# A graph attention kernel: two picked tiles in every batch from three bfloat16 parts, in place of one and two in turns from float32

## The chip, the core and the metric

The kernel runs on one core of a Trainium2 chip. The metric is the device time of one execution in microseconds (us), as the median of several runs; less is better. The profile is of one execution. The engines are named as the profile names them: PE is TensorE's matmuls and PEld its weight loads, DVE is VectorE, ACT is ScalarE, POOL is GpSimd, and SP is SyncE, which only issues DMAs.

## The reference

Three layers of a graph transformer on 6250 nodes of 64 numbers and 206250 directed edges (each edge in both directions and a loop at every node), sorted by their destination. Every edge has 64 numbers of its own. One layer is

```
def _transformer_conv(x, src, dst, edge_attr, Wq, bq, Wk, bk, Wv, bv, We, Ws, bs):
    q = x @ Wq + bq
    k = x @ Wk + bk
    v = x @ Wv + bv
    e = edge_attr @ We
    kj = k[src] + e
    alpha = jnp.sum(q[dst] * kj, axis=-1) / jnp.sqrt(jnp.float32(D))
    amax = jax.ops.segment_max(alpha, dst, num_segments=N)
    p = jnp.exp(alpha - amax[dst])
    denom = jax.ops.segment_sum(p, dst, num_segments=N)
    w = p / denom[dst]
    msg = (v[src] + e) * w[:, None]
    agg = jax.ops.segment_sum(msg, dst, num_segments=N)
    return agg + x @ Ws + bs

for i in range(L):                       # L = 3
    x = _transformer_conv(x, src, dst, edge_attr, Wq[i], bq[i], ...)
    x = jax.nn.relu(x)
    if i < L - 1:
        x = _layer_norm(x, ln_gamma[i], ln_beta[i])
return jax.nn.log_softmax(x, axis=1)
```

and the output is the layer norm of the input plus this. Everything is float32.

## The kernel before

**Tiles.** The edges are padded to 403 chunks of 512 (`CH`), each of four tiles of 128 edges (`T`). Four chunks are a batch (`LB`), so a batch has sixteen tiles and there are 101 batches, the last with three chunks. The nodes are 49 blocks (`NB`) of 128 rows. A batch lives in one buffer `feat` of six (`FB`): per edge the 64 numbers of the source node and the 64 of the edge. The edge half comes by one DMA on SP's queue (`fetch`). The node half is gathered: for each tile POOL issues one indirect DMA (`gather`, L542) that reads 128 rows of the layer's input from DRAM by the edges' sources.

**Picked tiles.** Some tiles at the end of a batch are not gathered but picked out of a copy of all node rows in SBUF (`xins`, 49 blocks of 128 rows in float32) by products with zeros and ones. `PICKS = (1, 2)`: batches pick one tile and two tiles in turns, beginning with batch 4 in the first layer. `keys` splits each source number into a key, which tells the bank of eight blocks and the row in a block, and the block within the bank. `aim` (L740) spreads one or two tiles' keys over all partitions by a product into the PSUM buffer `ps_p` (L746), and DVE compares them with the seven banks' row numbers (L751, seven operations) into the 0/1 matrices `hot`. `pick` (L754) then makes seven products a tile, one a bank, of 128 by 128 by 512 (the last one 64 wide), which add up in a PSUM buffer `ps_x` of two (L764); DVE keeps the right block of eight by a mask (L774) and a sum (L777), which writes the tile into `feat`. A float32 product shows in the profile as two matmuls, each with its own weight load.

**A round.** The main loop (L1127) is written out by hand and does one batch a round; each engine runs its instructions in the order in which they are issued there. In round u PE does: the sums of batch u-2 (`sums`, L1026, 32 matmuls of 32 columns), after which the buffer is free and POOL gathers batch u+4 into it (`room`); the transposed weights of batch u-1 (`weights`, L1018); the scores of batch u (`scores`, L999 and L1001), whose maximum DVE takes (L1006) and whose exponentials ACT makes (L1010); then the transposes of batch u+1's chunks in four turns (`turn`, L993 on PE, L994 on ACT into `featT`, six buffers). Between the turns stand the parts of `pick` for batch u+1, up to the fourth of the seven products after the first turn and the rest after the second, the same for a second tile around the third turn, and the `aim` for batch u+2 between the first two parts.

**Node work.** A generator is advanced by one step after every turn (`step`). `finish` (L855) closes a group of four blocks when all its edges are done: it merges two partial tables, multiplies by the value weights, normalises, stores the rows for the next layer's gathers and ends with `project` (L803) for the next layer, which makes the scaled queries (L812, L819), the skip part (L817) and a bias column (L824). In the first layer `begin` (L832) runs `project` on the input rows, which three DMAs (`enter`) load into `xins[0]` at the start. There are 13 groups in each layer. At a layer's end the node work is run out and POOL gathers the next layer's first six batches in a row.

Of the kernel before, what the change touches and what calls it, by code (L numbers as in the profile page):

```python
# [9 lines left out]
F32 = mybir.dt.float32  # L10
# [7 lines left out]
P = 128  # L18
D = 64
# [14 lines left out]
PICKS = (1, 2)  # L34
# [379 lines left out]
def main_path(  # L414
# [51 lines left out]

    nc = tc.nc
# [38 lines left out]
    xins = [inputs.tile([P, NB, D], F32, name="xin")]  # L506
    start = inputs.tile([P, NB, D], F32, name="xin").rearrange("p b d -> p (b d)")
    MOST = max(PICKS)

    def picked(layer, k):  # L510

        return PICKS[k % len(PICKS)] if batches[k][1] == LB and (layer or k >= LEAD) else 0

# [19 lines left out]
    def gather(layer, k):  # L533
# [3 lines left out]
        for c in range(m):  # L537
            for t in range(T):
                if m == LB and c * T + t >= LB * T - picked(layer, k):
                    continue  # L540
# [13 lines left out]
    assert NK * CH + 2 * NC <= NB * D  # L554
# [24 lines left out]
    def enter(b0, b1):  # L579
        nc.sync.dma_start(xins[0][:, b0:b1], x[b0 * P : b1 * P, :].rearrange("(j p) d -> p j d", p=P))  # L580

    enter(0, GS)
    enter(GS, 2 * GS)
    for k in range(FB):
        fetch(0, k)
        gather(0, k)
        if k == 1:
            enter(2 * GS, NB)
# [114 lines left out]
    keyT = const.tile([NT, MOST * P], F32, name="keyT")  # L703
    which = const.tile([P, MOST, NT, KB], BF16, name="which")
# [3 lines left out]
    def keys():  # L708
# [3 lines left out]
        key = turns.tile([P, MOST, NT], F32, name="key")  # L712
        low = turns.tile([P, MOST, NT], F32, name="low")
        h = turns.tile([P, 2, MOST, NT], F32, name="bits_of")
        tiles = src_b[:, : NT * LB * T].rearrange("p (k t) -> p t k", t=LB * T)
        nc.vector.tensor_copy(key, tiles[:, LB * T - MOST :, :])
# [17 lines left out]
        for s in range(MOST):  # L734
            nc.tensor.transpose(pt[:NT, s * P : (s + 1) * P], key[:, s, :], ident)
        nc.vector.tensor_copy(keyT, pt[:NT, : MOST * P])
# [3 lines left out]
    def aim(layer, k):  # L740

        if k >= len(batches) or not picked(layer, k):
            return
        n = picked(layer, k) * P
        pk = ps("p")[:, :n]
        nc.tensor.matmul(  # L746
            pk, ident[:NT, k : k + 1].to_broadcast([NT, P]), keyT[:, MOST * P - n :], start=True, stop=True
        )
        hot = picks.tile([P, NH, MOST * P], F32, name="hot")
        for h in reversed(range(NH)):  # L750
            nc.vector.tensor_scalar(hot[:, h, :n], pk, rank[:, h : h + 1], None, ALU.is_equal)  # L751
        hots[layer, k] = hot

    def pick(layer, k):  # L754

        if k >= len(batches) or not picked(layer, k):
            return
        hot = hots.pop((layer, k))
        n = picked(layer, k)
        for s in range(n):  # L760
            px = ps("x").rearrange("p (b d) -> p b d", b=KB)
            for h in range(NH):
                b0, b1 = h * KB, min((h + 1) * KB, NB)
                nc.tensor.matmul(  # L764
                    px[:, : b1 - b0, :].rearrange("p b d -> p (b d)"),
                    hot[:, h, s * P : (s + 1) * P],
                    xins[layer][:, b0:b1, :].rearrange("p b d -> p (b d)"),
                    start=(h == 0),
                    stop=(h == NH - 1),
                )  # L770
# [4 lines left out]
                rows, px, which[:, MOST - n + s, k, :].unsqueeze(2).to_broadcast([P, KB, D]), ALU.mult  # L775
            )
            nc.vector.tensor_reduce(  # L777
                loaded[layer, k][:, LB - 1, T - n + s, :D], rows.rearrange("p b d -> p d b"), AX.X, ALU.add
# [24 lines left out]
    def project(layer, g, n, y):  # L803

        pt = ps("a")
# [3 lines left out]
        nc.vector.tensor_copy(xT[:, : n * P], pt[:D, : n * P])  # L809
        yield  # L810
# [3 lines left out]
        nc.scalar.activation(qT[:, : n * P], pq[:D, : n * P], AF.Identity, bias=bqT[:, layer : layer + 1])  # L814
        pk = ps("g")[:, : n * (D + 1)].rearrange("p (j c) -> p j c", j=n)
# [7 lines left out]
        for j in range(n):  # L823
            nc.tensor.matmul(  # L824
                pk[:, j, D:], qT[:, j * P : (j + 1) * P], bkT[:, layer : layer + 1], start=True, stop=True
            )
        nc.vector.tensor_tensor(
# [4 lines left out]
    def begin(g, n):  # L832
        yield from project(0, g, n, xins[0][:, g : g + n])
# [21 lines left out]
    def finish(layer, g, n):  # L855
# [50 lines left out]
        if layer < L - 1:  # L906
            if g == 0:
# [326 lines left out]
```

## Time and profile before

| | |
|---|---|
| median of 3 runs | 7203.82 us (7203.37 to 7209.48) |
| the profiled execution's own time | 7203.82 us |
| its span, first to last instruction | 7202.1 us |
| mean granted TensorE clock | 0.831 |
| gathers by POOL, L542 | 4392 of 0.95 us each, one every 1.25 us |
| picked tiles, L774 | 444, with 6216 matmuls L764 |
| HBM read and written | 354.73 MB and 43.76 MB, 55 GB/s |

The profile gives for each engine the time in which it was busy. For a group of instructions it gives the line, engine, operation, what it writes and reads, the shapes, how many, the busy time in us, the mean of one in ns, and behind the bar the time for which the engine sat idle just before them and what ended most of that. "issue" means that nothing in the profile explains the wait, "remote" that its cause isn't in it. A timeline lists instructions in order of time (start, duration, engine, line), neighbours of one kind merged with their number (x8), and in brackets the idle time before them. A table of windows gives for each stretch its length, then for PE, PEld, DVE, ACT and POOL the busy time and the number of instructions, then the granted TensorE clock, the DMA engines' busy share and GB/s.

### The profile page before, as it was taken

Reading aid. Unit: us, or ns where it says so; the run is one execution under the profiler, and the core shown is the slowest. Engines: PE = TensorE matmul, PEld = TensorE weight load, DVE = VectorE, ACT = ScalarE, POOL = GpSimd, SP = SyncE. Lnnn points to the kernel's source line nnn. Section 1 sums busy time; section 2 is a strip of 40 time slices with the busy share of each in tenths; the row PEclk is TensorE's granted clock in tenths of the full one; section 3 lists DMA queues with packets and bytes.
Section 4 is the critical chain, followed back from the end, with each engine's and each line's share of the span. In section 5 each row is a group of like instructions: output and inputs, shape, how many; then the busy total and the mean of one; then the engine's idle time right before and its main releaser. Section 6 shows DMA issues by size and latency. Waiting matters only on the chain.

```text
span 7202.1 us, 83902 instructions
## 1 busy us (share of the span) xinstructions
PE 5175.8 (72%) x26605; PEld 2701.0 (38%) x26605; DVE 2315.1 (32%) x5431; ACT 1149.7 (16%) x2439; POOL 4165.8 (58%) x4400
## 2 busy tenths in 40 slices
PE   3877777777777657677777777774777777777776
PEld 2433333343333323333333343342333333333333
DVE  1433333333333223333333333331333333333333
ACT  0111111111111111111111111110111111111112
POOL 4455556566656355556656565535666666666663
PEclk9788888888888778888888888876888888888888
DMA  4322222222222212222222222221222222222222
GB/s 97 74 57 54 56 56 58 54 58 59 58 55 54 50 35 57 55 54 58 59 54 57 54 58 56 56 58 26 57 56 57 59 56 56 57 57 56 57 60 42
DMA packets 1098276, 404.43 MB, mean 56 GB/s; under 512 B 923557, under 2 KB 1022395, under 8 KB 1097826
## 3 DMA queue, kind: packets, MB, share of 16 engines
q1 hardware_dynamic: 941250, 246.60, 16.1%
q0 software_dynamic: 140544, 144.20, 10.5%
q10 hardware_dynamic: 16032, 8.17, 0.4%
q8 instruction: 216, 3.54, 0.2%
q14 instruction: 234, 1.92, 0.1%
HBM read 354.73 MB, written 43.76 MB: 55 GB/s over the span
## 4 chain that ended last, share of the span: by engine, by line


## 5 line engine op out<-in xcount | busy, mean ns | idle before, releaser
L542 POOL DMA_INDIRECT feat<-x,src_b x2750 | 2606.7, 948 | 1733.1 <-PE ps_g L1026 941.2
L764 PE MATMUL ps_x<-xin,hot 128*128 128x512 f32 x6216 | 2588.5, 560 | 49.3 <-issue 41.0
L542 POOL DMA_INDIRECT feat<-in_x,src_b x1375 | 1305.9, 950 | 957.6 <-PE ps_g L1026 560.9
L1026 PE MATMUL ps_g<-feat,probT 128*32 128x128 f32 x9672 | 814.9, 333 | 1362.5 <-issue 1335.3
L764 PEld LDWEIGHTS ps_x<-xin,hot 128*128 128x128 f32 x6216 | 1164.7, 197 | 1246.9 <-issue 1238.8
L994 ACT COPY featT<-ps_a 128x512 f32<-128x512 f32 x1209 | 677.4, 584 | 4378.8 <-remote 3335.0
L751 DVE TENSOR_SCALAR hot<-ps_p,rank 128x128 f32<-128x128 f32 (+1 forms) x2072 | 700.6, 409 | 1752.2 <-PE ps_a L993 709.6
L1026 PEld LDWEIGHTS ps_g<-feat,probT 128*32 128x32 f32 x9672 | 439.0, 127 | 1676.0 <-issue 1643.2
L774 DVE TENSOR_TENSOR rows_of_b<-ps_x,which 128x512 f32<-128x512 f32 x444 | 305.9, 689 | 2045.8 <-remote 1899.7
L993 PE MATMUL ps_a<-ident,feat 128*128 128x128 f32 x4836 | 767.0, 288 | 25.8 <-issue 25.8
L993 PEld LDWEIGHTS ps_a<-ident,feat 128*128 128x128 f32 x4836 | 587.4, 152 | 418.1 <-issue 365.3
L1001 PE MATMUL ps_s<-featT,q 128*32 128x512 f32 x2418 | 496.2, 840 | 126.7 <-ACT featT L994 65.0
L777 DVE TENSOR_REDUCE feat<-rows_of_b 128x64 f32<-128x512 f32 x444 | 460.2, 1037 | 15.3
L1010 ACT ACTIVATE prob<-ps_s,part 128x512 f32<-128x512 f32 (+2 forms) x306 | 210.2, 687 | 993.1 <-PE ps_a L993 359.7
L1018 PE MATMUL ps_p<-ident,prob 128*128 128x128 f32 (+2 forms) x1224 | 302.0, 394 | 23.0 <-ACT prob L1010 13.5
L1006 DVE TENSOR_REDUCE most<-ps_s 128x1 f32<-128x512 f32 (+2 forms) x306 | 210.4, 688 | 290.5 <-PE ps_s L1001 288.3
L542 POOL DMA_INDIRECT feat<-x,src_a x174 | 164.2, 943 | 232.6 <-PE ps_a L812 180.1
L1020 DVE COPY probT<-ps_p 128x512 f32<-128x512 f32 (+2 forms) x306 | 207.0, 676 | 190.8 <-PE ps_p L1018 189.6
L1018 PEld LDWEIGHTS ps_p<-ident,prob 128*128 128x128 f32 (+2 forms) x1224 | 195.2, 197 | 124.6 <-issue 48.4
L807 PE MATMUL ps_a<-ident,xin 128*64 128x128 f32 x147 | 38.1, 410 | 205.1 <-DVE xin L853 196.2
L999 PE MATMUL ps_s<-to,codeT 24*128 24x512 bf16 (+2 forms) x306 | 164.5, 537 | 4.2 <-issue 4.2
L1001 PEld LDWEIGHTS ps_s<-featT,q 128*32 128x32 f32 x2418 | 64.7, 128 | 271.9 <-issue 182.8
(123 smaller groups left out, 1706.3 us busy)
## 6 DMA issues: line engine op xcount, KB each, us to landing
feat<-in_ea SPq DMA_DIRECT2D x300, 512.0 KB
feat<-x,src_b POOLq DMA_INDIRECT x2750
feat<-in_x,src_b POOLq DMA_INDIRECT x1375
part<-part SPq DMA_DIRECT2D x1209, 16.2 KB
q<-qq SPq DMA_DIRECT2D x1209, 16.0 KB
both<-part SPq DMA_DIRECT2D x66, 260.0 KB
qq<-qs SPq DMA_DIRECT2D x33, 256.0 KB
to<-places SPq DMA_DIRECT2D x300, 24.0 KB
```

What stands on the lines that cost most here:

```text
L542: nc.gpsimd.indirect_dma_start(out=feat[:, c, t, :D], out_offset=None, in_=xts[layer][:, :], in_offset=bass.IndirectOffsetOnAxis(ap=index[ ...
L751: nc.vector.tensor_scalar(hot[:, h, :n], pk, rank[:, h : h + 1], None, ALU.is_equal)
L764: nc.tensor.matmul(px[:, : b1 - b0, :].rearrange("p b d -> p (b d)"), hot[:, h, s * P : (s + 1) * P], xins[layer][:, b0:b1, :].rearrange(" ...
L774: nc.vector.tensor_tensor(rows, px, which[:, MOST - n + s, k, :].unsqueeze(2).to_broadcast([P, KB, D]), ALU.mult)
L777: nc.vector.tensor_reduce(loaded[layer, k][:, LB - 1, T - n + s, :D], rows.rearrange("p b d -> p d b"), AX.X, ALU.add)
L993: nc.tensor.transpose(pt[:, t * P : (t + 1) * P], self.feat(j)[:, t, :], ident)
L994: nc.scalar.copy(featT, pt)
L1001: nc.tensor.matmul(self.p_s[j * W : (j + 1) * W, :], self.q[:, j, :], self.featT[j], start=False, stop=True)
L1006: nc.vector.tensor_reduce(top[:n], self.p_s[:n], AX.X, ALU.max)
L1010: nc.scalar.activation(self.prob[:n], self.p_s[:n], AF.Exp, bias=neg, accum_out=self.part[:n, P + 1 : P + 2])
L1018: nc.tensor.transpose(p_t[:, t, :n], self.prob[:n, t * P : (t + 1) * P], ident[:n, :n])
L1026: nc.tensor.matmul(p_g[j * W : (j + 1) * W, :P], self.probT[:, t, j * W : (j + 1) * W], self.feat(j)[:, t, :], start=(t == 0), stop=(t == ...
```

## The change

All full batches now pick two tiles (`PICKS = 2`). The node rows in SBUF are no longer float32 but three bfloat16 parts that add up to them (`parts`: high, mid, low; 3 x 49 blocks). `hot` becomes bfloat16, and `pick` makes three bfloat16 products a bank in place of one float32 product, 21 a tile. `project` makes the parts: ACT copies the rows to `high`; PE forms the rows minus `high` in PSUM by a product with the identity and one with its negative (`minus`), ACT copies that to `mid`; PE subtracts `mid`, and ACT copies the rest to `low`. These products use one of the two `ps_x` buffers. The input rows come by a DMA for each group (`rows_of`) in a step of their own in place of three DMAs at the start, the rows of later layers lie in a small tile `y`, and `featT` has five buffers in place of six. `pick` needs all groups' parts, so the loop runs the node work on until they are there before it picks for a layer's first batch. Where `aim` stands in the round is as before.

```diff
-PICKS = (1, 2)
+PICKS = 2
...
-    xins = [inputs.tile([P, NB, D], F32, name="xin")]
-    start = inputs.tile([P, NB, D], F32, name="xin").rearrange("p b d -> p (b d)")
-    MOST = max(PICKS)
+    parts = [inputs.tile([P, 3, NB, D], BF16, name="parts")]
+    start = inputs.tile([P, 3, NB, D], BF16, name="parts").rearrange("p s b d -> p (s b d)").bitcast(F32)
     def picked(layer, k):
-        return PICKS[k % len(PICKS)] if batches[k][1] == LB and (layer or k >= LEAD) else 0
+        return batches[k][1] == LB and (layer or k >= LEAD)
...
-                if m == LB and c * T + t >= LB * T - picked(layer, k):
+                if c * T + t >= LB * T - PICKS and picked(layer, k):
                     continue
...
-    def enter(b0, b1):
-        nc.sync.dma_start(xins[0][:, b0:b1], x[b0 * P : b1 * P, :].rearrange("(j p) d -> p j d", p=P))
-
-    enter(0, GS)
-    enter(GS, 2 * GS)
+    early = [rows_of(g, n) for g, n in groups[:2]]
     for k in range(FB):
         fetch(0, k)
         gather(0, k)
-        if k == 1:
-            enter(2 * GS, NB)
...
+    minus = const.tile([P, P], BF16, name="minus")
+    nc.vector.tensor_scalar(minus, ident, -1.0, None, ALU.mult)
...
     def aim(layer, k):
         if k >= len(batches) or not picked(layer, k):
             return
-        n = picked(layer, k) * P
-        pk = ps("p")[:, :n]
-        nc.tensor.matmul(
-            pk, ident[:NT, k : k + 1].to_broadcast([NT, P]), keyT[:, MOST * P - n :], start=True, stop=True
-        )
-        hot = picks.tile([P, NH, MOST * P], F32, name="hot")
+        pk = ps("p")[:, : PICKS * P]
+        nc.tensor.matmul(pk, ident[:NT, k : k + 1].to_broadcast([NT, P]), keyT, start=True, stop=True)
+        hot = picks.tile([P, NH, PICKS * P], BF16, name="hot")
         for h in reversed(range(NH)):
-            nc.vector.tensor_scalar(hot[:, h, :n], pk, rank[:, h : h + 1], None, ALU.is_equal)
+            nc.vector.tensor_scalar(hot[:, h, :], pk, rank[:, h : h + 1], None, ALU.is_equal)
         hots[layer, k] = hot
     def pick(layer, k):
...
-        for s in range(n):
+        for s in range(PICKS):
             px = ps("x").rearrange("p (b d) -> p b d", b=KB)
             for h in range(NH):
                 b0, b1 = h * KB, min((h + 1) * KB, NB)
-                nc.tensor.matmul(
-                    px[:, : b1 - b0, :].rearrange("p b d -> p (b d)"),
-                    hot[:, h, s * P : (s + 1) * P],
-                    xins[layer][:, b0:b1, :].rearrange("p b d -> p (b d)"),
-                    start=(h == 0),
-                    stop=(h == NH - 1),
-                )
+                for c in range(3):
+                    nc.tensor.matmul(
+                        px[:, : b1 - b0, :].rearrange("p b d -> p (b d)"),
+                        hot[:, h, s * P : (s + 1) * P],
+                        parts[layer][:, c, b0:b1, :].rearrange("p b d -> p (b d)"),
+                        start=(h == 0 and c == 0),
+                        stop=(h == NH - 1 and c == 2),
+                    )
                 if h == NH // 2:
                     yield
...
     def project(layer, g, n, y):
+        high, mid, low = (parts[layer][:, c, g : g + n, :] for c in range(3))
...
         nc.vector.tensor_copy(xT[:, : n * P], pt[:D, : n * P])
+        nc.scalar.copy(high, y)
         yield
...
         nc.scalar.activation(qT[:, : n * P], pq[:D, : n * P], AF.Identity, bias=bqT[:, layer : layer + 1])
+        pr = ps("x")[:, : n * D].rearrange("p (j d) -> p j d", d=D)
+        nc.tensor.matmul(pr, ident, y, start=True, stop=False)
+        nc.tensor.matmul(pr, minus, high, start=False, stop=True)
+        nc.scalar.copy(mid, pr)
...
+        nc.tensor.matmul(pr, minus, mid, start=False, stop=True, skip_group_check=True)
+        nc.scalar.copy(low, pr)
+        parted.add((layer, g))
...
-    def begin(g, n):
-        yield from project(0, g, n, xins[0][:, g : g + n])
+    def begin(g, n, y=None):
+        if y is None:
+            y = rows_of(g, n)
+            yield
+        yield from project(0, g, n, y)
...
-        if layer < L - 1:
-            if g == 0:
-                xins.append(inputs.tile([P, NB, D], F32, name="xin"))
-            y = xins[layer + 1][:, g : g + n]
-        else:
-            y = nodes.tile([P, GS, D], F32, name="y")[:, :n]
+        if layer < L - 1 and g == 0:
+            parts.append(inputs.tile([P, 3, NB, D], BF16, name="parts"))
+        y = nodes.tile([P, GS, D], F32, name="y")[:, :n]
...
-            featT = work.tile([P, CH], F32, name="featT", bufs=LB + 2)
+            featT = work.tile([P, CH], F32, name="featT", bufs=LB + 1)
...
         if picked(layer, 0):
-            assert all((layer - 1, g) in written for g, n in groups)
+            while not all((layer, g) in parted for g, n in groups):
+                advance()
             aim(layer, 0)
             for _ in pick(layer, 0):
                 pass
```

## The prediction

> **What bounds the kernel now.** I read the page first, then the PE and POOL timelines of two neighbouring rounds, then a table of the same rounds by windows.
>
> ```profile
> span 7202.1 us, 83902 instructions
> ...
> PE 5175.8 (72%) x26605; PEld 2701.0 (38%) x26605; DVE 2315.1 (32%) x5431; ACT 1149.7 (16%) x2439; POOL 4165.8 (58%) x4400
> ...
> L542 POOL DMA_INDIRECT feat<-x,src_b x2750 | 2606.7, 948 | 1733.1 <-PE ps_g L1026 941.2
> L764 PE MATMUL ps_x<-xin,hot 128*128 128x512 f32 x6216 | 2588.5, 560 | 49.3 <-issue 41.0
> ...
> L1026 PE MATMUL ps_g<-feat,probT 128*32 128x128 f32 x9672 | 814.9, 333 | 1362.5 <-issue 1335.3
> ```
>
> PE is the busiest, and half of it is the pick (L764). But PE also idles 1362.5 us in front of the sums (L1026), for "issue", and the gathers (L542) wait for those sums. So neither engine is simply full. The timelines of a round with one picked tile (POOL's first gather at 2980.16) show how it closes:
>
> ```profile
> 2987.20 2.05 PE L764 MATMUL ps_x<-xin,hot 128*128 128x512 f32 x6
> 2989.09 1.05 PE L993 MATMUL ps_a<-ident,feat 128*128 128x128 f32 x8
> 2990.06 0.64 PE L1026 MATMUL ps_g<-feat,probT 128*32 128x128 f32 x15
> 2992.18 0.27 PE L1026 MATMUL ps_g<-feat,probT 128*32 128x128 f32 x1 [1.48 <-issue]
> ...
> 3001.31 1.07 PE L1026 MATMUL ps_g<-feat,probT 128*32 128x128 f32 x11 [0.28 <-issue]
> ```
>
> ```profile
> 2997.62 0.94 POOL L542 DMA_INDIRECT feat<-x,src_b  x1 [0.30 <-issue]
> 3002.65 0.94 POOL L542 DMA_INDIRECT feat<-x,src_b  x1 [4.09 <-PE ps_g L1026]
> ```
>
> The sums start, crawl at one matmul in about 1.4 us, and run freely 2.75 us after the last gather's end (2998.56 to 3001.31). Their end then lets the next gathers go. The windows cut this round and the next (two tiles) at first gather, stall, release:
>
> ```profile
> 2980.16:2990.80 10.64, 10.54 (x60) 5.54 (x59) 5.03 (x11) 1.28 (x4) 8.20 (x9) 0.94 0.43 88
> 2990.80:3001.31 10.51, 2.07 (x7) 0.73 (x7) 0.70 (x2) 0.58 (x1) 5.93 (x7) 0.70 0.12 24
> 3001.31:3002.65 1.34, 1.34 (x13) 0.92 (x13) 1.28 (x2) 1.12 (x3) 0.00 (x1) 0.50 0.00 0
> 3002.65:3018.90 16.25, 16.01 (x61) 7.68 (x59) 3.88 (x11) 1.37 (x4) 12.29 (x14) 0.92 0.38 79
> 3018.90:3022.30 3.40, 0.48 (x2) 0.11 (x1) 0.00 (x0) 0.00 (x0) 0.91 (x1) 1.00 0.51 122
> 3022.30:3024.58 2.28, 2.21 (x31) 1.84 (x32) 2.04 (x5) 1.07 (x2) 0.00 (x0) 0.50 0.00 0
> ```
>
> Read the counts (PE, then its weight loads). From the first gather to the stall PE gets through 60 + 59 records in 10.6 us with one tile and 61 + 59 in 16.3 us with two: the same number, not the same time. The other engines stop too (DVE's next instruction waits 9.83 us for "remote", ACT's 6.57). So while POOL gathers, PE has an allowance of about 120 records, then 14 in 10.5 us, until some 2.6 us after the last gather. Which hardware does this the trace doesn't tell; I use it as found. PE's clock is 0.50 after the stall. Where POOL gathers nothing, a two-tile round takes 15.9 us (2390.50 to 2406.40), with no stall.
>
> By the starts of L999, one a round, 116 one-tile rounds free of node work take 22.56 us on average and 114 two-tile rounds 21.22, mean 21.89, though the latter have 5 us more of matmuls. The difference is one gather (1.25 us) and little else. These 230 rounds are 70% of the span.
>
> **The change, part by part.** The sum is made against the profiled execution, 7203.82 us (span 7202.1), which is also the median of the three runs.
>
> *Fewer gathers.* All 296 picked batches take two tiles, 148 gathers less, at 1.25 us from one to the next 185 us of POOL. It counts only in the former one-tile rounds: 14 gathers last 13 x 1.248 + 0.94 = 17.16 us, the release is then at 17.16 + 2.6 = 19.75 us.
>
> *The pick on PE.* A float32 product is two records 0.43 us apart (L764 x8 in 3.60 us): a tile is 12 x 0.43 + 2 short = 5.3 us. In bfloat16 it is 18 long and 3 short. The only bfloat16 row, L999, takes 0.39 us at full clock where an L764 record takes 0.59; 0.20 us less gives 0.22 us from one to the next, so 18 x 0.22 + 0.15 = 4.1 us a tile. The bounds are 0.20 and 0.43 (no faster). A round has 8.2 us of picks, in place of 5.3 and 10.6 in turns (mean 7.9). In PE time this is about nothing (592 x 4.1 against 444 x 5.3: +74 us, all where PE waits anyway). Going by records it is not: a tile is 21 matmuls with 21 loads, 42 in place of 28, and a round has 84 in place of 28 or 56.
>
> [...]
>
> *Where the allowance now ends.* PE's order from POOL's first gather, in matmuls: weights 4, scores 9, transposes 4, pick 12, keys 2, transposes 4, pick 9, transposes 4, pick 12: that is 60, with loads 120. Nine pick matmuls, four transposes and the 32 sums are still to come; in the two-tile round of today only the sums were. The stall comes at about 11.5 us, the crawl until 19.75 passes some 11 records. If the quicker pick gets more records through before the slow part begins, the stall is up to 10 records later; I take the middle. Left at the release: 0 to 4 pick matmuls (0 to 0.5 us, I take 0.2), four transposes (0.85 us at half clock, as L1018's four; 0.45 at full), 0.2 us of gap, the sums (29 took 1.94 us at half clock, so 32 take 2.15; 1.08 at full), 0.27 us to POOL. After a stall of 8 us the one-tile rows say half clock. So 19.75 + 3.65 = 23.4 us, between 21.75 (full clock, no pick left) and 24.0. Against 21.89 that is +1.5 us, times 230: **+347 us** (-32 to +485).
>
> [...]
>
> *Picks on DVE.* One more L774 and L777 (0.69 + 1.04 us) in former one-tile rounds, and always the wide L751 (7 in 2.83 us, 1.90 before). All rounds are then as the two-tile ones on DVE, which hides this behind the gathers; without that cover 2.7 us in every second round. L751 in bfloat16: same length (-1 to 0 us a round, hidden).
>
> *Splitting the rows (project), 39 groups.* Each adds a two-record float32 product, two bfloat16 products (eight records with loads), three ACT copies of 256 elements (about 0.4 us each by L930's 0.42) and holds one of the two ps_x buffers until the last copy. Its second half comes after turn 0, ahead of the pick, so the first tile takes the one buffer and the second tile waits for ACT's last copy, whose release comes late in the slow part. Behind PE's wait in its queue are the second tile, two sets of transposes and the sums, and POOL waits for those. The 22 such rounds of layers 1 and 2 (mean 23.87 us) then do the second tile after the release: +4.5 us (0 to 8.2, a tile at half clock), **+100 us**. The 22 rounds in front of them, which wait for norm on DVE (mean 28.3), and layer 2's 11 finishing rounds: +1 us each for records (0 to +3), **+33 us**.
>
> *Start.* The one load of rows becomes eleven, on SP's queue in order, 0.4 us each, and a step more a group; the two node rounds at 158 and 195 us (36.5 and 27.9 us) get 11 groups x (0.9 us PE, 1.2 ACT), half beside other work: **+20 us** (0 to +40). *Layer borders:* 84 gathers in place of 87, twice: **-7 us**. The second tile picked there lies under the 105 us of gathers. *featT, 5 buffers for 6:* nothing; the scores that free a buffer stand ahead of its next turn in PE's order, and if ACT's copy came late it would be 0.6 us a round. *minus, y apart from the inputs:* nothing, one DVE operation at the start and a tile in another place.
>
> Sum: 347 + 100 + 33 + 20 - 7 = +493, so **7695 us**, +6.8%. With the ends of its terms it lies between 7250 and 7900.
>
> **Rivals.** *A, the allowance isn't of records* (faster). If the stall goes by time, bytes or the place in the round, each round becomes a two-tile round of today: (21.22 - 21.89) x 230 = -154, node rounds 0 to +50, start +20, borders -7: 7060 to 7130, taken 7095. For it: one-tile and two-tile rounds run the same instructions up to their second transposes, so equal counts may be an equal place. Against: in the one the count ends 15 sums in, in the other just as the sums begin. It decides where the sums still begin before the stall. *B, one weight load serves the three products of a key half.* Then a round has 56 pick records as now and PE is 2.4 us shorter: 7060 to 7130 as in A. Against: every matmul of the page has its load (26605 and 26605). *C, all of the second tile waits in every round*, for a buffer or for late keys (L751 started 3 to 5 us after its product): the tile at half clock costs up to 8.2 us after the release in place of 0.2, a part of it in the crawl; +2.5 us more a round, 7695 + 575 = 8270. Against: both ps_x buffers are free within 4 us of the first gather.
>
> **How the numbers follow.** The forecast 0.65, A 0.20, B 0.05, C 0.10. The range leaves out C (0.10) and the lower half of A (0.10): 7090 to 7900; the forecast alone 7250 to 7900. A change of 0.2% is about what can be told from none here. Slower: forecast and C, less 0.01 for a sum that happens to cancel; faster: A and B less 0.01: 0.74, 0.02 same, 0.24.
>
> **What would show it.** Right: 84 pick records a round, PE's first idle "issue" now in front of L764, not L1026, some 120 records after the first gather; POOL's idle before its first gather 6 us where it was 4.1; plain rounds near 23.4; second tiles behind ACT's copy in node rounds. Wrong: stalls still at L1026 and POOL idle at 4 to 4.5 us (A or B, told apart by the count of loads), or rounds of 26 us (C). The prediction fails first if the 120 is a place and not a count.

## The result and the profile after

The changed kernel takes 7498.62 us (median of 4 runs, 7494.4 to 7502.97) against 7203.59 us for the kernel before, run beside it (7194.56 to 7209.48): a ratio of 1.0411, with a 95% interval of 1.0393 to 1.0429. It is slower by 295 us, where 491 us were forecast. The profiled execution took 7494.5 us.

In the changed kernel gathers stand at L543, the pick at L759, the sums at L1031, the transposes at L998, the scores at L1004 and L1006. The page of the kernel after has these lines (groups: operation, tiles, shapes, number | busy us, mean ns | idle us before them, and what ended most of it):

```profile
span 7492.7 us, 97063 instructions
...
PE 5240.4 (70%) x32977; PEld 2764.9 (37%) x32977; DVE 2715.0 (36%) x5728; ACT 1223.2 (16%) x2556; POOL 4038.2 (54%) x4252
...
L759 PE MATMUL ps_x<-parts,hot 128*128 128x512 bf16 (+1 forms) x12432 | 2869.1, 367 | 1636.0 <-issue 1432.8
L543 POOL DMA_INDIRECT feat<-x,src_b x2656 | 2525.7, 951 | 2000.5 <-PE ps_g L1031 1248.1
...
L1031 PE MATMUL ps_g<-feat,probT 128*32 128x128 f32 x9672 | 559.2, 397 | 30.9 <-issue 26.6
```

PE's unexplained idle time has changed its place. Before, 1335.3 us of "issue" stood in front of the sums; now 26.6 stand there, and 1432.8 in front of the pick. POOL has 148 gathers less and is busy for 4038.2 us in place of 4165.8, but it waits longer for the sums (1248.1 us on the costliest line, 941.2 before). The PE timeline of a plain round shows how it closes now (start us, duration, line, number, idle before):

```profile
2846.79 2.75 PE L759 MATMUL ps_x<-parts,hot 128*128 128x512 bf16 x12
...
2852.10 2.97 PE L759 MATMUL ps_x<-parts,hot 128*128 128x512 bf16 x13
2856.07 0.39 PE L759 MATMUL ps_x<-parts,hot 128*128 128x512 bf16 x1 [0.99 <-issue]
2857.49 0.38 PE L759 MATMUL ps_x<-parts,hot 128*128 128x512 bf16 x1 [1.04 <-issue]
...
2863.83 0.32 PE L759 MATMUL ps_x<-parts,hot 128*128 128x64 bf16 x3 [0.16 <-issue]
2863.96 1.09 PE L998 MATMUL ps_a<-ident,feat 128*128 128x128 f32 x4
2864.98 1.94 PE L1031 MATMUL ps_g<-feat,probT 128*32 128x128 f32 x32
```

POOL's timeline, the last gather of this round and the first of the next:

```profile
2860.32 0.94 POOL L543 DMA_INDIRECT feat<-x,src_b  x1 [0.30 <-issue]
2867.22 0.95 POOL L543 DMA_INDIRECT feat<-x,src_b  x1 [5.95 <-PE ps_g L1031]
```

The second tile runs thirteen products, then crawls at one in about 1.4 us. It runs freely at 2863.83, that is 2.57 us after the last gather's end (2861.26). Transposes and sums, 3.0 us of work, still lie ahead, and POOL waits 5.95 us where it waited 4.09. The windows of this round, cut at first gather, stall, release and next gather (length, then PE, PEld, DVE, ACT, POOL busy and number, PE clock, DMA share, GB/s):

```profile
2844.09:2855.00 10.91, 10.91 (x61) 5.42 (x59) 1.96 (x4) 1.28 (x4) 8.47 (x9) 0.95 0.43 87
2855.00:2863.80 8.80, 2.59 (x6) 0.43 (x6) 2.83 (x7) 0.00 (x0) 4.75 (x6) 0.72 0.13 24
2863.80:2867.22 3.42, 3.39 (x41) 2.61 (x42) 3.13 (x4) 1.90 (x4) 0.00 (x0) 0.50 0.00 0
```

Up to the stall PE got 61 matmuls and 59 loads through, the 120 of the kernel before. The third window is the new cost: 41 matmuls with their loads at a clock of 0.50.

By the starts of the score product, one a round, 229 plain rounds (no node work) now take 23.11 us on average, where 230 took 21.89. That is +1.22 x 230 = +281 us of the 291 us between the two profiled executions.

### The profile page after: what moved, and what is told of

Its sections match the earlier page's. It is cut to its first block, busy times and chain, and to the rows that moved or that the text cites. A ratio compares the mean times of both kernels' runs of the same rounds, so it can differ in the third digit from the quotient of the medians.

```text
span 7492.7 us, 97063 instructions
## 1 busy us (share of the span) xinstructions
PE 5240.4 (70%) x32977; PEld 2764.9 (37%) x32977; DVE 2715.0 (36%) x5728; ACT 1223.2 (16%) x2556; POOL 4038.2 (54%) x4252
## 4 chain that ended last, share of the span: by engine, by line
## 5 line engine op out<-in xcount | busy, mean ns | idle before, releaser
L759 PE MATMUL ps_x<-parts,hot 128*128 128x512 bf16 (+1 forms) x12432 | 2869.1, 367 | 1636.0 <-issue 1432.8
L543 POOL DMA_INDIRECT feat<-x,src_b x2656 | 2525.7, 951 | 2000.5 <-PE ps_g L1031 1248.1
L759 PEld LDWEIGHTS <-hot 128*128 128x128 bf16 x12432 | 1208.5, 100 | 3076.0 <-issue 2071.4
L543 POOL DMA_INDIRECT feat<-in_x,src_b x1328 | 1265.2, 953 | 1105.0 <-PE ps_g L1031 728.5
L745 DVE TENSOR_SCALAR hot<-ps_p,rank 128x256 bf16<-128x256 f32 x2072 | 838.5, 476 | 1882.6 <-remote 1006.2
L998 PE MATMUL ps_a<-ident,feat 128*128 128x128 f32 x4836 | 917.9, 312 | 265.9 <-issue 258.5
L769 DVE TENSOR_TENSOR rows_of_b<-ps_x,which 128x512 f32<-128x512 f32 x592 | 407.9, 689 | 1840.6 <-remote 1251.0
L998 PEld LDWEIGHTS ps_a<-ident,feat 128*128 128x128 f32 x4836 | 617.8, 157 | 721.9 <-issue 673.2
L772 DVE TENSOR_REDUCE feat<-rows_of_b 128x64 f32<-128x512 f32 x592 | 616.5, 1041 | 20.6
L1031 PE MATMUL ps_g<-feat,probT 128*32 128x128 f32 x9672 | 559.2, 397 | 30.9 <-issue 26.6
L1031 PEld LDWEIGHTS ps_g<-feat,probT 128*32 128x32 f32 x9672 | 401.5, 160 | 163.7 <-issue 131.0
L1006 PE MATMUL ps_s<-featT,q 128*32 128x512 f32 x2418 | 383.7, 691 | 1.3 <-ACT featT L999 1.3
L543 POOL DMA_INDIRECT feat<-x,src_a x168 | 158.9, 946 | 236.3 <-PE ps_a L810 185.7
L742 PE MATMUL ps_p<-keyT,ident 100*128 100x256 f32 x592 | 178.3, 382 | 2.6 <-DVE parts L672 1.3
L1004 PE MATMUL ps_s<-to,codeT 24*128 24x512 bf16 (+2 forms) x306 | 150.1, 491 | 0.0
## 6 DMA issues: line engine op xcount, KB each, us to landing
part<-part SPq DMA_DIRECT2D x1209, 16.2 KB
```

What stands on the lines that cost most here:

```text
L543: nc.gpsimd.indirect_dma_start(out=feat[:, c, t, :D], out_offset=None, in_=xts[layer][:, :], in_offset=bass.IndirectOffsetOnAxis(ap=index[ ...
L745: nc.vector.tensor_scalar(hot[:, h, :], pk, rank[:, h : h + 1], None, ALU.is_equal)
L759: nc.tensor.matmul(px[:, : b1 - b0, :].rearrange("p b d -> p (b d)"), hot[:, h, s * P : (s + 1) * P], parts[layer][:, c, b0:b1, :].rearran ...
L769: nc.vector.tensor_tensor(rows, px, which[:, s, k, :].unsqueeze(2).to_broadcast([P, KB, D]), ALU.mult)
L772: nc.vector.tensor_reduce(loaded[layer, k][:, LB - 1, T - PICKS + s, :D], rows.rearrange("p b d -> p d b"), AX.X, ALU.add)
L998: nc.tensor.transpose(pt[:, t * P : (t + 1) * P], self.feat(j)[:, t, :], ident)
```

## The experiments

Two theories stand against each other. **Count**: while POOL gathers, PE may issue a fixed number of records, and the changed pick uses up 84 of them in place of 28 or 56. **Place or length**: what is given is a time, bytes, or a place in the round, and the change loses in some other way. All runs but three were made on chips where the kernel before takes 7197 to 7215 us.

### Two float32 tiles in every batch

The gathers left out, without the bfloat16 parts. On the kernel before:

```diff
-PICKS = (1, 2)
+PICKS = (2,)
```

> The kernel before with two tiles picked in every batch and still in float32: the gathers of the change alone (14 a round), with 56 pick records a round. Theory 'count' (from POOL's first gather PE gets some 122 records through, then crawls until 2.6 us after the last gather): every plain round becomes today's two-tile round, 21.2 us in place of 21.9 on average, so 7050 us (7020 to 7090). Rival 'place' (the stall sits at a place in the round's program) and rival 'length' (it comes after so much time of matmuls): the same, 7050. If fewer gathers bring nothing: 7200.

Measured: 7116.02 us (7092.66 to 7123.9), ratio 0.988 (0.9839 to 0.9921). The page has the stall back at the sums, half of what it was there, and little in front of the pick:

```profile
L764 PE MATMUL ps_x<-xin,hot 128*128 128x512 f32 (+1 forms) x8288 | 3378.2, 553 | 109.7 <-remote 64.7
...
L1026 PE MATMUL ps_g<-feat,probT 128*32 128x128 f32 x9672 | 697.1, 348 | 739.3 <-issue 729.3
```

So leaving out the gathers gains, as the rival A would have it, and the loss comes with the parts. The time lies outside the expected 7020 to 7090, 66 us above its middle. Plain rounds take 21.69 us, not the 21.22 of the two-tile rounds before: next gathers come 4.45 us after the last one's end, where the two-tile rounds had 4.12.

### Two of the three parts

On the changed kernel, the third product of each bank is left out (the low part is made, but not added):

```diff
-                for c in range(3):
+                for c in range(2):
...
-                        stop=(h == NH - 1 and c == 2),
+                        stop=(h == NH - 1 and c == 1),
```

> The changed kernel with the products of the third part (low) left out of the pick, so that a tile is 14 matmuls with 14 loads and a round has 56 pick records in place of 84; the part is still made. The output loses the lowest bits of picked rows. 'Count': the stall moves from the pick back to the sums, plain rounds 21.2 us in place of 23.1, so 7498 - 229 x 1.9 = 7060 us (7010 to 7130). 'Place' (the stall sits in the second tile's pick because of what bfloat16 or the parts bring there): 7400 to 7500. 'Length': less than 7100 too, since the pick is shorter.

Measured: 7127.02 us (7118.54 to 7140.22), ratio 0.9898 (0.9861 to 0.9935). With 56 pick records a round it is the kernel of 7116 us again, although its pick is 1798.0 us of PE and that one's 3378.2:

```profile
L759 PE MATMUL ps_x<-parts,hot 128*128 128x512 bf16 (+1 forms) x8288 | 1798.0, 361 | 246.2 <-issue 188.9
L1031 PE MATMUL ps_g<-feat,probT 128*32 128x128 f32 x9672 | 919.9, 390 | 1598.4 <-issue 1578.0
```

1580 us less of PE time changes nothing: a good half of it reappears as stall in front of the sums (1598.4 us against 739.3). The node work with the splitting of the rows is still in this kernel, so it can't be what costs 295 us.

### More records, no more work

On the kernel of 7116 us, the first tile's six full float32 products are cut in two halves of 256 columns: 24 records more, the same columns. The picked numbers come out different from the whole products'; why, the runs don't tell, and only the time is read here.

```diff
+                for m0, m1 in ((0, 4), (4, 8)) if s == 0 and b1 - b0 == KB else ((0, b1 - b0),):
                     nc.tensor.matmul(
-                        px[:, : b1 - b0, :].rearrange("p b d -> p (b d)"),
+                        px[:, m0:m1, :].rearrange("p b d -> p (b d)"),
...
-                        xins[layer][:, b0:b1, :].rearrange("p b d -> p (b d)"),
+                        xins[layer][:, b0 + m0 : b0 + m1, :].rearrange("p b d -> p (b d)"),
```

> As e1_two_f32, but the first tile's products are cut into two halves of 256 columns: the same arithmetic, the same columns streamed, 84 pick records a round in place of 56. 'Count': the stall moves into the second tile's pick as in the changed kernel, plain rounds 23.1 to 23.8 us, 2.1 us over e1, so 7050 + 230 x 2.1 = 7530 us (7400 to 7650). 'Length' and 'place': as e1, 7050 (7030 to 7100).

Measured: 7499.68 us (7493.97 to 7502.53), ratio 1.0421 (1.0383 to 1.0458), the time of the changed kernel, in float32. Plain rounds take 22.93 us, and the stalls move forward from the sums into the second tile and the transposes:

```profile
L765 PE MATMUL ps_x<-xin,hot 128*128 128x256 f32 (+2 forms) x11840 | 3558.1, 445 | 578.9 <-issue 500.0
...
L995 PE MATMUL ps_a<-ident,feat 128*128 128x128 f32 x4836 | 881.3, 298 | 525.8 <-issue 508.7
L1028 PE MATMUL ps_g<-feat,probT 128*32 128x128 f32 x9672 | 553.3, 387 | 88.0 <-issue 80.8
```

Rounds in which POOL gathers nothing take 15.95 us here and 15.93 in the kernel of 7116 us (medians): the cut costs PE nothing by itself.

### Records without columns

The same 24 records as six float32 products of one column, ahead of the first tile, which then overwrites what they write:

```diff
+            for _ in range(6 if s == 0 else 0):
+                nc.tensor.matmul(
+                    px[:, 0, :1], hot[:, 0, :P], xins[layer][:, 0, :1], start=True, stop=True
+                )
```

The first run fell on another chip (below). The second:

> Two float32 tiles in every batch and 6 one-column float32 products a round, again, for the same reason. With stalls, if records are counted: 7500 us (7430 to 7570), plain rounds 22.9 us, 118 to 128 records at the stall. If time, bytes or place is counted: 7116 to 7220. Without stalls: 5753 us again, where the products cost their own time on PE.

Measured: 7549.95 us (7519.79 to 7561.2), ratio 1.0498 (1.047 to 1.0527); plain rounds 22.90 us. A PE timeline of a round whose first gather starts at 2780.54 and whose last ends at 2797.73:

```profile
2784.12 1.40 PE L763 MATMUL ps_x<-xin,hot 128*128 128x1 f32 x12
2785.38 3.68 PE L768 MATMUL ps_x<-xin,hot 128*128 128x512 f32 x8
...
2792.10 3.60 PE L768 MATMUL ps_x<-xin,hot 128*128 128x512 f32 x8
2796.73 0.59 PE L768 MATMUL ps_x<-xin,hot 128*128 128x512 f32 x1 [1.03 <-issue]
2798.12 0.59 PE L768 MATMUL ps_x<-xin,hot 128*128 128x512 f32 x1 [0.81 <-issue]
2800.22 1.66 PE L768 MATMUL ps_x<-xin,hot 128*128 128x512 f32 x4 [1.51 <-issue]
```

Six products of one column (twelve matmuls, twelve loads) do what halving six products did: 22.90 against 22.93 us a round. They take 1.3 us of PE, more than the 0.5 put down for them (the author's estimate), so by themselves they would not exclude a count of time; the halves, which take none, do.

Over these kernels the stall can be put in one table. Taken is the first step of over 0.65 us between two PE records after the sixtieth, in plain rounds, counted from POOL's first gather (medians):

| kernel | PE records up to the stall | at us |
|---|---|---|
| before, rounds with one picked tile | 118 | 10.31 |
| before, rounds with two | 118 | 16.22 |
| two float32 tiles | 120 | 16.07 |
| two of the three parts | 114 | 10.54 |
| halves | 126 | 14.13 |
| one-column products | 127 | 15.51 |
| after | 122 | 11.21 |
| three tiles, two parts (below) | 123 | 11.12 |

The number stays within 114 to 127 while the time runs from 10.3 to 16.2 us, and within the kernel before both kinds of rounds stop at 118, 5.9 us apart. That is a count, though not an exact one: in half of the changed kernel's plain rounds it lies between 118 and 125, in a quarter of those with three tiles at 111 or less. On the pages every matmul has a weight load of its own (26605 of each in the kernel before, 32977 in the changed one), so the rows don't tell whether it is records, matmuls or loads that are counted.

### Whose count it is

On the kernel of 7116 us, 24 fills of one column on DVE at the start of each pick:

```diff
+        for _ in range(24):
+            nc.vector.memset(spare, 0.0)
```

> Two float32 tiles in every batch (7116 us on a chip whose rounds stall) and 24 fills of one column on DVE each round, again, since the first run of it fell on a chip without stalls. With stalls, if the allowance belongs to PE's own instructions: 7080 to 7180, the stall at the sums after 118 to 128 PE records. If all engines share one allowance: 7400 to 7600, the stall about 24 PE records earlier. Without stalls: 5497 us again.

Measured: 7226.47 us (7203.59 to 7241.73, 10 runs), ratio 1.0038 (1.0019 to 1.0057), outside both expected ranges. Against the 0.988 of the same kernel without the fills it costs 1.6%, under a third of what 24 PE records cost (5.5 and 6.3%). PE stalls after 117 records at 15.69 us, as without them, though 24 DVE records more have gone before. So DVE's records don't count against PE's allowance, but the fills are not free, and the reason is on DVE's timeline, where POOL's first gather starts at 2915.05:

```profile
2919.25 2.08 DVE L762 MEMSET spare<- 128x1 f32 x17
2922.05 0.18 DVE L762 MEMSET spare<- 128x1 f32 x2 [0.72 <-DVE spare L762]
2922.79 0.06 DVE L762 MEMSET spare<- 128x1 f32 x1 [0.55 <-DVE spare L762]
2923.49 0.18 DVE L762 MEMSET spare<- 128x1 f32 x2 [0.64 <-DVE spare L762]
```

DVE stalls too, after a median of 24 of its own records and 7.06 us after the first gather, when PE has made only 52; its fills, each waiting for nothing but the one before, then come one or two at a time, mostly 0.7 us apart. But 24 is no fixed number of DVE's, as PE's 120 is. In the plain round of the changed kernel shown above (first gather at 2844.09) DVE and ACT are held after three records each:

```profile
2847.29 0.15 DVE L1013 TENSOR_SCALAR part<-most 128x1 f32<-128x1 f32 x1
2856.10 2.83 DVE L745 TENSOR_SCALAR hot<-ps_p,rank 128x256 bf16<-128x256 f32 x7 [8.66 <-remote]
```

```profile
2848.21 0.58 ACT L999 COPY featT<-ps_a 128x512 f32<-128x512 f32 x1
2863.87 1.07 ACT L999 COPY featT<-ps_a 128x512 f32<-128x512 f32 x2 [15.08 <-remote]
```

What they wait for was done on PE at 2849.98 (the keys' product) and 2850.41 (the transposes), 5.9 and 6.3 us after the first gather, and the fills run back to back until 6.3 us after it. For these two engines the rows fit a time of some 6 us better than a count of their own records, but no run was made to separate the two. DVE's seven comparisons then run without a pause while POOL still gathers.

Plain rounds lose only 0.2 us by it (21.89 against 21.69, 46 us); the 22 rounds ahead of the ones with `project`, which wait for DVE's norm (in the kernel before, 196.2 us of PE's idle time are put down to it), lose 2.8 us each (28.68 against 25.86, 62 us), together 108 of the 110 us.

### Fewer gathers

On the changed kernel, eight gathers a round; the other six tiles come by two plain DMAs on SP's queue, from other rows.

```diff
+                if c < 2 and t < 3 and k >= FB:
+                    if t == 0:
+                        nc.sync.dma_start(
+                            feat[:, c, :3, :D], xts[layer][: 3 * P, :].rearrange("(t p) d -> p t d", p=P)
+                        )
+                    continue
```

> The changed kernel with 8 gathers a round in place of 14 from the seventh batch of a layer on: six tiles are filled by two plain DMAs on SP's queue with rows that are not the right ones, so the output is not the reference's. PE's records are unchanged. 'Count', with the gathers as what holds PE up: the gathers end at 9.7 us, the release comes at 12.3, about when the allowance ends, and a plain round takes 13.5 to 15 us, close to PE's own 13.1 without gathers; 5400 us (5300 to 5900). If the stall has another cause than the gathers, the rounds stay above 20 us and the time above 6900.

Measured: 5146.21 us (5145.87 to 5146.54), ratio 0.715 (0.7116 to 0.7183). Of 226 plain rounds 171 have no stall of PE and take 13.41 us, where rounds without gathers take 13.25; the other 55 take 14.18. With 84 pick records in place, the stall is gone: it is the gathers that make it. Expected was 5400 (5300 to 5900), with some crawl left, and the time lies below that; eight gathers end 9.7 us after the first, when PE has made a median of 112 records, so that it hardly meets the limit. ACT is held all the same. In the timeline of one round, whose first gather starts at 2914.91, ACT makes three copies in a row 1.78 us after the last gather's end (2924.60), and the transposes for the first of them had ended 5.8 us earlier (2920.55):

```profile
2919.95 0.60 PE L1004 MATMUL ps_a<-ident,feat 128*128 128x128 f32 x4
...
2923.66 0.94 POOL L549 DMA_INDIRECT feat<-x,src_b  x1 [0.30 <-issue]
...
2926.38 1.56 ACT L1005 COPY featT<-ps_a 128x512 f32<-128x512 f32 x3 [7.52 <-remote]
```

### The split rows' PSUM bank

In the changed kernel, `project`'s remainders in the scores' bank, so that no `ps_x` buffer is held:

```diff
-        pr = ps("x")[:, : n * D].rearrange("p (j d) -> p j d", d=D)
+        pr = ps("s")[:, : n * D].rearrange("p (j d) -> p j d", d=D)
```

> The changed kernel with project's products of the remainders in the scores' bank, again, since its first run fell on a chip without stalls. With stalls, if the second tile's wait for ACT's last copy costs the node rounds what the changed kernel shows above the kernel before: the 22 rounds with project fall from 25.7 or 25.9 us to 24.0 to 24.8 and the total by 20 to 40 us, to 7440 to 7485. If the wait costs nothing: these rounds stay at 25.3 to 26.3, the total at 7485 to 7520. If the scores wait for the bank instead: over 26.3 and over 7520. Without stalls: 5473 us again.

Measured: 7491.49 us (7484.45 to 7494.61), ratio 1.038 (1.036 to 1.0399). The 22 rounds with `project` take 24.95 us, between the two expectations, where the changed kernel has 25.69 and, in a second run of it, 25.89: 0.74 to 0.94 us a round less, 16 to 21 us in all. The total is 7 to 11 us lower, where the changed kernel's own two medians differ by 3.4, and lies where it was expected if the wait costs nothing. Nor can the difference be read as the price of the wait, for the clock differs as well. From 2.6 us after the last gather's end to the end of the round, the granted clock is 1.00 in 21 of the 22 rounds with the other bank, but only in 9 of the changed kernel's (8 in its second run). At full clock the changed kernel's rounds take 24.0 us on average and those with the other bank 24.9. So what the edit gains goes with the clock. Why that differs, and what the wait costs by itself, no run shows. In the changed kernel's trace the wait is there, but rare. The ACT and PE timelines of one such round, whose last gather ended at 3194.34:

```profile
3196.86 0.37 ACT L830 CAST parts<-ps_x 128x256 bf16<-128x256 f32 x1 [10.69 <-PE ps_a L998]
...
3197.28 3.11 PE L759 MATMUL ps_x<-parts,hot 128*128 128x512 bf16 x7 [1.57 <-ACT parts L830]
```

ACT's last copy, ready since 3186.5, is made after the release, and PE's second tile starts within 0.1 us of its end. That is so in four of the 22 rounds, and in five in the second run. Of the idle times in front of the pick, all rounds of the changed kernel taken together, only two are put down to that copy (what ended the wait: us in total, times), beside the 2941 for which nothing shows:

```profile
  issue: 3504.2, 2941
...
  ACT parts L830: 2.4, 2
```

### Three tiles from two parts

If records and gathers are both what counts, they can be traded. On the changed kernel, three tiles a batch from the high and middle parts; the low part is not made, and a tile's products are no longer split between two turns:

```diff
-PICKS = 2
+PICKS = 3
...
-                for c in range(3):
+                for c in range(2):
...
-                if h == NH // 2:
-                    yield
...
-        nc.tensor.matmul(pr, minus, mid, start=False, stop=True, skip_group_check=True)
-        nc.scalar.copy(low, pr)
```

> The changed kernel with three tiles picked in place of two, each from the high and middle parts alone (the low part, of relative size 2 to the power -16, is left out and not made): 84 pick records a round, as in the changed kernel, but 13 gathers in place of 14. With stalls: the release comes 1.25 us earlier and the same records are left, so plain rounds 23.1 - 1.25 = 21.9 us and 7499 - 287 = about 7200 (7100 to 7280). Without stalls POOL bounds the round with 13 x 1.25 = 16.25 us in place of 17.5: about 5200 (5120 to 5320).

Measured: 7143.83 us (7137.74 to 7149.33), ratio 0.9926 (0.99 to 0.9952). Plain rounds take 21.90 us, the 21.9 worked out from the release (13 gathers, 15.96 us) and the 84 records. The account by count and release gives the round before it is run. The total is 56 us under the 7200 named with it, for the 22 rounds with `project` are shorter too (23.96 us against 25.69). But the third tile, a gather less for 28 records more, gains nothing on two tiles of two parts (7127 us).

### A chip without the stall

The first runs of three of these kernels fell on another chip:

> Two float32 tiles in every batch (the kernel of 7116 us), with 24 fills of one column (128x1) put on DVE at the start of each round's pick; TensorE's instructions are those of the 7116 us kernel. If the allowance belongs to PE's own instructions: 7116 us, within 7080 to 7180, stall still at the sums. If all engines share one allowance, 24 records of it are gone and the rounds go as with 24 more records on PE (7500 us): 7400 to 7600, stall in the second tile or the turns.

> The changed kernel, with project's products of the remainders in the bank of the scores in place of one of the two ps_x banks; nothing else is different. If the second tile waits for ACT's last copy in the node rounds, as the prediction said, the 22 rounds with project in layers 1 and 2 fall from 25.7 us to 24.0 to 24.8 and the total by 20 to 40 us, to about 7465 (7445 to 7490). If that wait costs nothing (the records alone do): the same rounds stay at 25.3 to 26.1 and the total at 7498 (7485 to 7515). If the scores then wait for the bank: over 26 and over 7515.

> Two float32 tiles in every batch (7116 us), with 6 float32 products of one column put ahead of the first tile's own, into the same bank, which the tile then overwrites: 24 records more, by count as the kernel with halved products (7500 us), but almost no TensorE time (about 0.5 us a round at most) and no length. If records are what is counted: 7500 us again (7430 to 7570), plain rounds 22.9, records at the stall 118 to 128. If time, bytes or a place in the round is counted: 7116 to 7180, stall at the sums.

The kernel before took 5653.79 us there (5647.01 to 5662.46), at a gather still of 0.95 us, one every 1.25 us. Two float32 tiles with the fills on DVE took 5497.29 us (ratio 0.9728, 0.9711 to 0.9745), the changed kernel with the other bank 5472.95 us (0.9678, 0.9659 to 0.9698), the one-column products 5752.91 us (1.0173, 1.0156 to 1.019). None of the expectations holds, as all were written for rounds that stall. The page and the timelines of the run with fills on DVE:

```profile
PE 5184.2 (94%) x28677; PEld 2776.5 (51%) x28677; DVE 3101.6 (56%) x12831; ACT 1196.2 (22%) x2439; POOL 4033.3 (73%) x4252
```

```profile
2208.59 0.60 PE L996 MATMUL ps_a<-ident,feat 128*128 128x128 f32 x4
2209.12 1.08 PE L1029 MATMUL ps_g<-feat,probT 128*32 128x128 f32 x32
...
2209.35 0.94 POOL L542 DMA_INDIRECT feat<-x,src_b  x1 [0.30 <-issue]
2210.27 0.27 ACT L1037 COPY part<-ps_g 128x128 f32<-128x128 f32 x1 [0.40 <-PE ps_g L1029]
2210.59 0.95 POOL L542 DMA_INDIRECT feat<-x,src_b  x1 [0.30 <-issue]
```

The sums take 1.08 us while POOL gathers (in the windows of two such rounds, 1973.0 to 2004.8, the granted clock is 1.00), ACT follows 0.40 us after them, and POOL goes from one batch into the next without waiting. Here PE is the bound with float32 (15.90 us in most rounds) and the gathers are with bfloat16 parts (16.96 us on average, 14 x 1.25 = 17.5 where they set it). The one-column products, which on the stalling chips cost what the halves cost, here cost their own PE time: 17.25 us a round against 15.90 in most rounds with fills.

On this chip the change itself was not run. With the other bank, which on the stalling chips differs from it by some 0.1%, it is 3.2% faster than the kernel before. That the change would then also be faster there is argued, not shown.

The changed kernel was run once more:

> The changed kernel again, to set beside the runs of a chip on which the kernel before took 5654 us in place of 7204 and no round stalls. On a chip of the first kind: 7499 us (7480 to 7520), ratio 1.04. On one of the second kind, where the allowance does not exist, records cost nothing and the gathers left out count: 5475 us (5440 to 5520) against 5654, ratio 0.968.

On a chip that stalls it took 7502.0 us (7495.4 to 7518.38), ratio 1.0424 (1.0396 to 1.0451), plain rounds 23.15 us.

## Why the prediction was right, and where its sizes were off

The mechanism is the one predicted for the plain rounds, and its marks are there: 84 pick records a round, the first "issue" in front of the pick and not the sums, about 120 records after the first gather, POOL waiting 5.83 us (median) where it waited about 4. One mark is mostly missing, second tiles behind ACT's copy in the rounds with `project`.

*The stall.* Predicted after 120 records, or by the author's estimate up to 10 later, at about 11.5 us; measured 122 at 11.21. *The release.* Predicted 19.75 us after the first gather; measured 17.20 + 2.53 = 19.73. *From the release to the next gather.* Predicted 3.65 us, measured 5.83 - 2.53 = 3.30. The sums were put at 2.15 us (32 times what 29 had taken) and a gap of 0.2 added; in the round shown they take 1.94 and there is no gap. The four transposes were put at 0.85 us; they take 1.02 until the sums start. A plain round is therefore 23.11 us, not 23.4, and the **term of the plain rounds** +281 us, not +347.

*The pick on PE.* A bfloat16 product was put at 0.22 us: 12 in 2.75 us, the last one 0.38 long, are 0.215 us from one to the next. A quicker one would have mattered little: the two-part kernel, with 1580 us less of PE time than the kernel of 7116 us at the same count, takes 7127.

*The project rounds*, **+100 us**, are the step that failed by the largest ratio: 22 rounds went from 23.87 to 25.69 us, +40. The step took the whole second tile to lie behind the release, held by ACT's last copy, and priced it at 4.5 us, about half of a tile at half clock. Counted from 2.6 us after the last gather's end, 10 to 21 of the tile's 21 products do lie behind the release, 16 on average. But the tile starts on the copy's end in only four of the 22 rounds, and half clock holds for a part of the time at most. In nine rounds the granted clock is 1.00 from there on, and they take 23.2 to 24.3 us; in the other 13 it is 0.64 to 0.81, and they take 25.9 to 27.2. Here are the products behind the release in one round of each kind, and the windows from there to the next round:

```profile
477.83 5.92 PE L759 MATMUL ps_x<-parts,hot 128*128 128x512 bf16 x17 [0.82 <-issue]
...
4963.10 3.06 PE L759 MATMUL ps_x<-parts,hot 128*128 128x512 bf16 x16 [0.34 <-issue]
```

```profile
477.83:485.79 7.96, 7.96 (x58) 3.79 (x57) 6.19 (x11) 1.93 (x4) 0.26 (x1) 0.66 0.04 8
...
4963.10:4968.19 5.09, 5.09 (x57) 3.03 (x57) 4.82 (x10) 1.93 (x4) 0.25 (x1) 1.00 0.07 16
```

And a part of the price was in the 23.87 us already: the 12 rounds of this kind that picked two tiles before had 6 to 12 pick matmuls behind the release, and took 24.6 us.

*The rounds before them and the finishing ones*, +33: 22 x (27.31 - 28.27) = -21 and about 0. They wait for DVE's norm anyway (196.2 us of PE's idle time in the kernel before, 100.7 in the changed one), and had one gather less in half of the cases; the step added records to rounds whose end another engine sets. *Start*, +20: the first score product comes 3.7 us earlier and the two node rounds together take 4.0 longer, so 0. *Layer borders*, -7: the two stuck rounds with 84 gathers take 158.7 and 159.3 us against 157.3 and 158.3, so nothing is gained from three gathers fewer; the rounds after them are 2.5 us shorter each, together -3.

With these, 281 + 40 - 21 - 3 gives +297 us, beside the 291 measured. Four of the five terms were put too high, all in one direction: the plain rounds for the sums' length, the project rounds for the clock, and the other two for work that lies under something else. The ends of the range, 7250 and 7900, are not the sums of the terms' own ends, which give 7165 and 8001.

*The rivals.* A, that the allowance is no count, falls with the halves and the one-column products; B, shared weight loads, with 32977 matmuls and 32977 loads; C, all of the second tile behind the release, with plain rounds of 23.11 us. What no rival had was a chip on which there is no allowance. There the forecast's first step is void.

## What to carry to other kernels

Where PE stalls beside a stream of indirect DMAs as here, count its instructions, not their time. On the chips that stall, cutting a product in two (7499.68 us) or splitting it into bfloat16 parts (7498.62) cost the same for the same 84 pick records a round, and about halving the pick's PE time at the same 56 (3378.2 to 1798.0 us) gained nothing (7116 and 7127). If a saving in gathers is the aim, take it alone: two float32 tiles in every batch beat both kernels on a chip that stalls, with 7116 us against 7204 and 7499. On the other chip the same kernel with extra DVE work beat the kernel before (0.9728), but the changed kernel with the other bank beat it by a little more (0.9678). And measure on more than one chip before a stall is designed around, since the kernel before takes 7204 us where PE stalls and 5654 on the chip where it doesn't, about a fifth less.

## What the runs showed of the hardware

While POOL issues gathers, one every 1.25 us, PE gets some 120 records through from the first gather on, matmuls and their weight loads together (medians of 114 to 127 over eight kinds of rounds, reached after 10.3 to 16.2 us). Then it goes on slowly, with 12 records in 8.80 us in the changed kernel's round shown, until about 2.5 us after the last gather's end (a median of 2.53, 2.57 in that round). ACT and DVE are held too. In the rounds shown, work that was ready for them 5.6 to 6.3 us after the first gather was not begun then, while DVE's fills ran on until 6.3; ACT had made 3 records of its own in one round, DVE 3 in one and a median of 24 in another kernel, and a count is not shown for them. Eight gathers in a row instead of fourteen, 9.7 us, keep PE out of it in 171 of 226 rounds, but not ACT in the round shown.

This holds in four of the five sets of runs and not in the fifth, on another chip, where the gathers, at the same 0.95 us, hold up no engine in the timelines shown, and the kernel before takes 5654 in place of 7204 us. What differs between them the traces don't tell, nor which hardware gives the allowance. Every execution timed here also recorded its spans; there is none without that to compare.
